# Attention over four images on one core: later column sums, a third forms buffer, one bias product, a new end, and matmul operands 320 bytes apart

## The chip, the core and the metric

The kernel runs on one core of a Trainium2 chip. A core has a matrix engine (PE, with its weight loads shown apart as PEld), a vector engine (DVE), an activation engine (ACT), a general engine (POOL) and a queue engine (SP). SP, ACT and POOL can also start DMA transfers. Each engine works through its own instructions in the order in which the program lists them, and semaphores make one engine wait for another. The metric is the time of one execution on the device, in microseconds (us).

## The reference

For each of B = 4 images with N = 64 * 64 = 4096 positions and C = 256 channels:

```python
q = x @ Wq + bq            # (N, 128)
k = x @ Wk + bk            # (N, 128)
v = x @ Wv + bv            # (N, 256)
pq, pk, pv = (t.reshape(B, -1, N) for t in (q, k, v))   # a reinterpretation of memory, no transpose
energy = einsum('bcn,bcm->bnm', pq, pk)                 # (N, N)
attention = softmax(energy, axis=-1)
out = einsum('bcm,bnm->bcn', pv, attention).reshape(x.shape)
result = gamma * out + x
```

All is float32. The kernel works without subtracting a maximum before the exponential. At its end it tests whether every column sum stayed within bounds, and a slower general path, behind a branch on that flag, would recompute everything. With these inputs the branch is not taken.

## The kernel before

**Forms.** A float32 operand of a matmul is split into three forms that the matrix engine reads in its rounded float32 type: h (the upper part, made by ACT), l (the rest) and d (a combination for the crossed terms), both made by DVE. A product of two numbers is then three matmuls, summed in PSUM: first the d forms, then, after the partial sum has been rescaled in place (`seed_qk`, `seed_v`, `cross`), the h and the l forms.

**Image 0** is projected first, in a loop over NI = 16 blocks `i` of 256 positions. The loop body is written out by hand, and this order holds on each engine:

- PE: `products(0, i, 0, (0, 1))` (8 matmuls for q and k), `products(0, i, 1, (0, 1))` (8 for v), then for block i + 1 the 4 d matmuls of q and k, the bias products `biased` (4 matmuls of a 128 x 128 tile of ones with the two forms of the bias), the 4 d matmuls of v, and 4 transposes of block i + 2.
- ACT: `qk_forms` (L268), `v_forms` (L152), `seed_qk` (L251), then `x_forms` of block i + 2 (L209) and, behind it, `seed_v` (L260, two instructions).
- DVE: two instructions each of `qk_forms` (L271) and `v_forms` (L155), then two of `x_forms` (L211, L213).
- POOL: four stores per block of the forms of q and k to DRAM (`store`, L290), and loads of q and k for the attention.

The forms of q and k of one block live in tile `f` of the ring `pf`, which has two buffers; L268 of block i overwrites the buffer of block i - 2, so it waits for that block's four stores.

**Attention** runs in B * 128 = 512 steps `n`; 16 steps (t = 0 to 15) make a group of 512 columns, and eight groups an image. On PE one step is `cross(n + 2)` (2 matmuls, L318), `attend(n, 0)` (6 matmuls, L378), `energy(n + 2)` (4 matmuls, L333) and `attend(n, 1)` (6 matmuls). ACT makes the rescaling (L319), the exponential (L336) and h (`upper`, L342); DVE the running column sum (L351), l (L356) and d (L358) in `halves(n + 1)`. Into the steps of images 0 to 2, `step` interleaves the projection of the next image: 24 product matmuls of 128 x 256 (L229) for each of its 16 blocks.

At the end of a group, ACT copies the accumulators out of PSUM (`emptied`, L392: half 0 in the last step, half 1 afterwards), PE adds the column sums over the partitions (`sums`, two matmuls, L416, into a bank that an accumulator of half 1 has held), and `finish` takes twelve pieces, one per step: the sums go through DRAM, are inverted, the output tile `o` is added up and multiplied, a POOL DMA adds x (L442) and an SP DMA stores the result (L446). In the last image `late` is 1: half 1 is emptied at t = 1 of the next group, and `sums` stands in the same step, right behind it.

`finish_last` is the end of the last group: column sums by four small float32 matmuls (`zp`, L459), reciprocal, a broadcast by a float32 matmul (`rp`, L478), the test of all sums (`np`, L481, and the flag `again`, L494), the scaling of the two halves and two stores (L488, L493). The branch on `again` (L675) follows.

Of the kernel before, what the change touches and what calls it, by code (L numbers as in the profile page):

```python
# [20 lines left out]
def kernel(  # L21
# [36 lines left out]
    nc = tc.nc  # L58
# [28 lines left out]
    LOOK = 2  # L87
    xg, og = columns(x, NB), columns(out, NB)
# [4 lines left out]
    again = const.tile([P, 1], I32, name="again")  # L93
    gam3 = const.tile([P, 3], F32, name="gam")
    gam, gam1, gam2 = (gam3[:, i : i + 1] for i in range(3))
    zs = const.tile([P, 1], F32, name="zs")
    rall = const.tile([P, B * NG, NJ], F32, name="rall")
    bias = const.tile([P, 2 * C2], F32, name="bias")
    bvs = const.tile([P, KC], F32, name="bvs")

    with ExitStack() as fast:
# [3 lines left out]
        )  # L105
        qkv = pool("qkv", 1)
# [10 lines left out]
        wf = qkv.tile([P, 2, 3, KC, C], F32R, tag="wf", name="wf")  # L117
# [32 lines left out]
        def split(h, l, d, y, scale=E):  # L150

            nc.scalar.activation(h, y, AF.Identity, scale=UPPER * scale)  # L152
            yield
            for t, f in ((d, 1.0 / scale + 1.0), (l, 1.0 / scale)):
                nc.vector.scalar_tensor_tensor(t, h.bitcast(F32), -f, y, ALU.mult, ALU.add)  # L155
                yield

        def weights(w):

            nc.scalar.mul(scaled[:, w], raw[:, w], E ** -(w + 1))  # L160
            yield from split(*(wf[:, w, f] for f in range(3)), scaled[:, w])
# [54 lines left out]
        def products(b, i, w, fs):  # L216
# [5 lines left out]
            for s in range(2):  # L222
                for f in fs:
                    for k in range(KC):
                        if w:
                            left, right = wf[:, 1, f, k, s * P : (s + 1) * P], xf[:, f, k]
                        else:
                            left, right = xf[:, f, k, s, :], wf[:, 0, f, k]
# [9 lines left out]
        def biased(i):  # L238

            to = units[0, 0, i]  # L240
            for f in range(2):
                for s in range(2):
                    nc.tensor.matmul(  # L243
                        to[:, s, :], ones_r, bf[:, f, :], start=False, stop=False,
                        skip_group_check=True,
                    )
# [17 lines left out]
        def qk_forms(b, i):  # L264
            y = units.pop((0, b, i))
            f = work.tile([P, 2, 3, C], F32R, tag="pf", name=f"f_{b}_{i}")
# [78 lines left out]
        def halves(n):  # L345
# [6 lines left out]
            else:  # L352
                now["s"] = x
            ld = ppool.tile([P, 2, 2, NB], F32R, tag="ld", name=f"ld_{n}")
# [6 lines left out]
            if n % NU == NU - 1:  # L361
                nc.vector.tensor_tensor(s[:, 0, :], s[:, 0, :], s[:, 1, :], ALU.add)
                now["sum"] = s
# [89 lines left out]
        def finish_last(n, xr):  # L453

            b, g = B - 1, NG - 1
            attend(n, 0)
# [21 lines left out]
            nc.tensor.matmul(rp, ones, work_[:, 0], start=True, stop=True)  # L478
# [408 lines left out]
```

## Time and profile before

| | us |
|---|---|
| median of 3 runs | 2398.16 (2396.82 to 2399.83) |
| the profiled execution | 2397.88 |
| its span, first to last instruction | 2396.1 |

Between the span and that execution's own time lie 1.8 us. A page of the profile gives the busy time of each engine, its share of the span, the costliest groups of instructions, and DMA. Other views answer questions about one stretch: a table of windows (busy time of each engine, the granted share of the PE clock, DMA), a timeline (start, duration, engine, line, output and inputs, how many instructions; in brackets the idle time before it and what ended it), and the chain of waits, followed back from the last instruction. A merged timeline row with xN spans from the start of the first of N instructions to the end of the last. PE matmuls are pipelined: one lasts longer than the distance to the next, so the spacing of N equal matmuls is (row's duration - one matmul's) / (N - 1).

### The profile page before, as it was taken

How to read it: one execution, taken by the hardware profiler on the slowest of the kernel's cores; microseconds unless marked ns; L12 is line 12 of the kernel's file. 1: busy time of each engine (PE TensorE's matmuls, PEld its weight loads, DVE VectorE, ACT ScalarE, POOL GpSimd, SP SyncE). 2: the span in 40 equal slices, each digit the busy share in tenths (PEclk: the TensorE clock that was granted, in tenths of full speed). 3: DMA queues.
4: the chain of work that ended last, by engine and by line, in shares of the span. 5: the costliest groups of instructions: out<-in, count | busy, mean ns of one | idle time of the engine just before them, and what ended most of it. 6: DMA issues, size and time to landing. Idle time of an engine off the chain costs nothing.

```text
span 2396.1 us, 31995 instructions
## 1 busy us (share of the span) xinstructions
PE 2355.5 (98%) x11158; PEld 1967.6 (82%) x11158; DVE 2135.3 (89%) x2111; ACT 1882.2 (79%) x3093; POOL 580.7 (24%) x943
## 2 busy tenths in 40 slices
PE   8999999999999999999999999999999999999998
PEld 7888888888888888888888888888888787777776
DVE  6889999999999999999999999999998888888887
ACT  6777788887888887888877888878887777777775
POOL 5422222222322222222232222222223111111110
PEclk9999999999999999999999999999999999999999
DMA  9857666567896576566697665676669545445443
GB/s 216 177 139 199 169 165 171 144 174 183 262 274 163 147 187 178 157 166 156 164 342 220 159 175 142 175 188 156 167 175 337 134 128 128 126 111 129 114 124 88
DMA packets 243991, 413.83 MB, mean 173 GB/s; under 512 B 26031, under 2 KB 141487, under 8 KB 243822
## 3 DMA queue, kind: packets, MB, share of 16 engines
q0 software_dynamic: 203152, 368.77, 59.2%
q1 hardware_dynamic: 40126, 42.67, 5.7%
q8 instruction: 91, 1.49, 0.3%
q14 instruction: 78, 0.64, 0.1%
q10 hardware_dynamic: 544, 0.26, 0.0%
HBM read 306.64 MB, written 104.98 MB: 172 GB/s over the span
## 4 chain that ended last, share of the span: by engine, by line
PE 96%; ACT 2%; DVE 1%; DMA 1%; issue 0%; POOL 0%; SPq 0%; ACTq 0%; DVEq 0%
PE a L378 39%; PE b L378 19%; PE e L333 19%; PE e L318 10%; PE qv L229 7%; PE xt L198 1%; PE z L416 1%; ACT x L336 0%; ACT o L392 0%; DMA qd<-f 0%; ACT qv L260 0%; DMA raw<-in_L_conv_Wv_dram 0%; PE qv L243 0%; ACT xf L209 0%; DVE ld L358 0%
## 5 line engine op out<-in xcount | busy, mean ns | idle before, releaser
L336 ACT ACTIVATE x<-e 128x512 f32<-128x512 f32 x960 | 522.0, 596 | 301.7 <-PE e L333 295.4
L305 POOL DMA_DIRECT2D k<-kf x512 | 275.5, 538 | 1738.3 <-PE e L333 1678.3
L356 DVE TENSOR_TENSOR ld<-x,h 128x1024 fp32r<-128x1024 f32 x480 | 586.0, 1221 | 100.5 <-ACT h L342 55.8
L351 DVE TENSOR_TENSOR s<-s,x 128x1024 f32<-128x1024 f32 x480 | 586.5, 1222 | 99.7 <-ACT x L336 97.5
L378 PE MATMUL a<-h,v 128*128 128x512 f32 x2048 | 642.9, 395 | 0.0
L319 ACT ACTIVATE e<-e 128x512 f32<-128x512 f32 x1024 | 546.4, 572 | 119.7 <-PE e L318 119.3
L378 PE MATMUL b<-ld,v 128*128 128x512 f32 x2048 | 632.7, 390 | 1.7 <-DVE f L271 1.5
L378 PE MATMUL a<-ld,v 128*128 128x512 f32 x2048 | 633.8, 391 | 0.0
L358 DVE SCALAR_TENSOR_TENSOR ld<-h,x 128x1024 fp32r<-128x1024 f32 x480 | 584.7, 1218 | 0.0
L333 PE MATMUL e<-q,k 128*128 128x512 f32 x2048 | 547.7, 389 | 0.0
L342 ACT ACTIVATE h<-x 128x1024 fp32r<-128x1024 f32 x480 | 510.5, 1064 | 13.2
L378 PEld LDWEIGHTS b<-ld,v 128*128 128x128 f32 x2048 | 384.8, 188 | 84.6 <-issue 1.9
L378 PEld LDWEIGHTS a<-ld,v 128*128 128x128 f32 x2048 | 385.4, 188 | 83.4
L333 PEld LDWEIGHTS e<-q,k 128*128 128x128 f32 x2048 | 384.2, 188 | 79.7
L378 PEld LDWEIGHTS a<-h,v 128*128 128x128 f32 x2048 | 369.5, 189 | 70.6 <-ACT o L392 7.3
L318 PE MATMUL e<-q,k 128*128 128x512 f32 x1024 | 316.2, 390 | 0.0
L318 PEld LDWEIGHTS e<-q,k 128*128 128x128 f32 x1024 | 192.2, 188 | 40.8
L229 PEld LDWEIGHTS qv<-xf,wf 128*128 128x128 f32 x768 | 107.5, 191 | 17.9 <-ACT qv L260 8.0
L229 PE MATMUL qv<-xf,wf 128*128 128x256 f32 x768 | 114.5, 285 | 7.2 <-ACT qv L260 5.4
L229 PE MATMUL qv<-wf,xf 128*128 128x256 f32 x768 | 114.9, 286 | 3.6 <-DVE xf L211 1.9
L229 PEld LDWEIGHTS qv<-wf,xf 128*128 128x128 f32 x768 | 108.1, 192 | 12.7 <-ACT qv L251 2.6
L290 POOL DMA_DIRECT2D kf<-f x128 | 98.3, 768 | 29.1 <-DVE f L271 6.9
(84 smaller groups left out, 1230.4 us busy)
## 6 DMA issues: line engine op xcount, KB each, us to landing
k<-kf POOLq DMA_DIRECT2D x512, 384.0 KB, 3.6
vf<-vf POOLq DMA_DIRECT2D x48, 768.0 KB, 5.3
v<-vf POOLq DMA_DIRECT2D x48, 768.0 KB, 8.3
kf<-f POOLq DMA_DIRECT2D x128, 192.0 KB, 4.4
qd<-f POOLq DMA_DIRECT2D x128, 192.0 KB, 4.4
q<-qd POOLq DMA_DIRECT2D x32, 768.0 KB, 5.2
o<-in_x_dram POOLq DMA_DIRECT2D x31, 512.0 KB, 7.4
out_dram<-o SPq DMA_DIRECT2D x31, 512.0 KB
```

Of the source, the lines that this page charges most:

```text
L229: nc.tensor.matmul(to[:, s, :], left, right.rearrange("p s a -> p (s a)") if w else right, start=(f == 2 and s == k == 0), stop=(f == 1 an ...
L290: nc.gpsimd.dma_start(to, f)
L305: nc.gpsimd.dma_start(t, kf[b, u % NU])
L318: nc.tensor.matmul(e, *forms(n, i, 2), start=True, stop=False, skip_group_check=True)
L319: nc.scalar.mul(e, e, -REST)
L333: nc.tensor.matmul(e, *forms(n, i, f), start=False, stop=(f == 1), skip_group_check=True)
L336: nc.scalar.activation(x[:, i, :], e, AF.Exp, scale=(1.0 + E) ** 3 / E)
L342: nc.scalar.activation(h, units[n], AF.Identity, scale=UPPER)
L351: nc.vector.tensor_tensor(s, s, x, ALU.add)
L356: nc.vector.tensor_tensor(l, x, h.bitcast(F32), ALU.subtract)
L358: nc.vector.scalar_tensor_tensor(d, h.bitcast(F32), 1.0 + E, x, ALU.mult, ALU.subtract)
L378: nc.tensor.matmul(to, vall[:, t, f, i, j * P : (j + 1) * P], units[n][f][:, i, :], start=(t == 0 and i == 0 and f != 1), stop=(t == NU - ...
```

## The change

- `sums` and the start of `finish` move in the last image from t = 1 to t = 2 of the next group (`t == 2 * late`).
- In image 0 the forms of every third block go into a third tile, `f3`, which is the not yet used first buffer of the ring `q`.
- `biased` issues 2 matmuls rather than 4: the bias's upper part stands in partition 0 and its rest in partition 32 of one 64-row operand that is zero elsewhere.
- In the loop of image 0, `seed_v(0, i + 1)` stands right behind its products, ahead of the transposes and of `x_forms(0, i + 2)` on ACT.
- At the start, the scaling of the raw weights moves from ACT to DVE, and ACT makes h from the raw weights.
- The matmuls of `products` run over forms, then contraction halves, then output halves `s` (before: `s` outermost).
- Tiles move: the weights' forms become two tiles, small tiles stand between them, and x's forms get their own pool behind 192 bytes of padding (in image 0 they start 192 bytes into the buffer `ld`). By the addresses of the built programs, stationary minus moving operand of `products` was a multiple of 512 bytes and is 320 bytes modulo 512 afterwards. All other matmuls of the attention keep a multiple of 512; the tile of ones stood and stands 384 (modulo 512) from the bias's form and from the forms of the column sums.
- The end: the last column sum is added up ahead of the last l and d; the small matmuls, the broadcast and the test stand ahead of both last `attend` halves or between them; the flag `again` is computed before the last multiplications, and each engine reads it at the end of its own work; the last half takes one DVE instruction less.

```diff
+    PAD = 48
...
+        wf = [pool("wqk", 1).tile([P, 3, KC, C], F32R, name="wqkf")]
+        small = pool("small", 1)
...
+        wf.append(pool("wv", 1).tile([P, 3, KC, C], F32R, name="wvf"))
...
+        pool("pad", 1).tile([P, PAD], F32, name="pad")
+        xpool = pool("xf", 1)
...
         def weights(w):
-            nc.scalar.mul(scaled[:, w], raw[:, w], E ** -(w + 1))
-            yield from split(*(wf[:, w, f] for f in range(3)), scaled[:, w])
+            y, c = scaled[:, w], E ** -(w + 1)
+            nc.vector.tensor_scalar(y, raw[:, w], c, None, ALU.mult)
+            h, l, d = (wf[w][:, f] for f in range(3))
+            nc.scalar.activation(h, raw[:, w], AF.Identity, scale=UPPER * E * c)
...
             if b == 0:
-                f = ppool.tile([P, 3, KC, 2, P], F32R, tag="ld", name=f"xf_{b}_{i}")
+                f = ppool.tile([P, PAD + 6 * C], F32R, tag="ld", name=f"xf_{b}_{i}")
+                f = f[:, PAD:].rearrange("p (f k s a) -> p f k s a", f=3, k=KC, s=2)
             else:
-                f = work.tile([P, 3, KC, 2, P], F32R, tag="xf", name=f"xf_{b}_{i}", bufs=1)
+                f = xpool.tile([P, 3, KC, 2, P], F32R, tag="xf", name=f"xf_{b}_{i}")
...
-            for s in range(2):
-                for f in fs:
-                    for k in range(KC):
+            for f in fs:
+                for k in range(KC):
+                    for s in range(2):
...
         def biased(i):
-            for f in range(2):
-                for s in range(2):
-                    nc.tensor.matmul(
-                        to[:, s, :], ones_r, bf[:, f, :], start=False, stop=False,
-                        skip_group_check=True,
-                    )
+            for s in range(2):
+                nc.tensor.matmul(
+                    to[:, s, :], ones_r[:64], bf[:64], start=False, stop=False,
+                    skip_group_check=True,
+                )
...
+            if b == 0 and i % 3 == 2:
+                f = f3
+            else:
+                f = work.tile([P, 2, 3, C], F32R, tag="pf", name=f"f_{b}_{i}")
...
+            if n == B * STEPS - 1:
+                whole()
             ld = ppool.tile([P, 2, 2, NB], F32R, tag="ld", name=f"ld_{n}")
...
         def finish_last(n, xr):
-            attend(n, 0)
             zp = ps_e.tile([P, NJ], F32, tag="e", name="zp")
...
+            attend(n, 0)
             emptied(n, 0)
             o = now["o"]
-            attend(n, 1, (2,))
             rp = ps_e.tile([P, NB], F32, tag="e", name="rp")
             nc.tensor.matmul(rp, ones, work_[:, 0], start=True, stop=True)
-            attend(n, 1, (0, 1))
             np_ = ps_p.tile([P, 1], F32, tag="p0", name="np")
             nc.tensor.matmul(np_, ones, zs, start=True, stop=True)
-            nc.scalar.activation(o[:, 1, 1, :], now["b", 1], AF.Identity, scale=gam1)
+            attend(n, 1, (2, 0, 1))
             r = work.tile([P, NB], F32, tag="r", name="r_last", bufs=1)
             nc.scalar.copy(r, rp)
+            nc.scalar.activation(o[:, 1, 1, :], now["b", 1], AF.Identity, scale=gam1)
             nc.vector.tensor_tensor(o[:, 0, 0, :], o[:, 0, 0, :], o[:, 1, 0, :], ALU.add)
+            nc.vector.tensor_scalar(again, np_, P - 0.5, None, ALU.is_lt)
...
-            nc.vector.tensor_tensor(o[:, 1, 1, :], o[:, 1, 1, :], r, ALU.mult)
-            nc.vector.tensor_tensor(xr[:, 1, :], xr[:, 1, :], o[:, 1, 1, :], ALU.add)
-            nc.vector.scalar_tensor_tensor(o[:, 0, 1, :], now["a", 1], gam2, r, ALU.mult, ALU.mult)
-            nc.vector.tensor_tensor(xr[:, 1, :], xr[:, 1, :], o[:, 0, 1, :], ALU.add)
+            y = o[:, 1, 1, :]
+            nc.vector.scalar_tensor_tensor(y, now["a", 1], gam2, y, ALU.mult, ALU.add)
+            nc.vector.tensor_tensor(y, y, r, ALU.mult)
+            nc.vector.tensor_tensor(xr[:, 1, :], xr[:, 1, :], y, ALU.add)
             nc.sync.dma_start(og[b, g][:, 1], xr[:, 1, :])
-            nc.vector.tensor_scalar(again, np_, P - 0.5, None, ALU.is_lt)
...
+        f3 = work.tile([P, 2, 3, C], F32R, tag="q", name="f3")
...
                 products(0, i + 1, 1, (2,))
+                seed_v(0, i + 1)
             if i + 2 < NI:
                 transposed(0, i + 2)
                 xs = x_forms(0, i + 2)
                 next(xs)
-            if i + 1 < NI:
-                seed_v(0, i + 1)
...
-            if t == late and n > 1:
-                sums(n - 1 - late)
+            if t == 2 * late and n > 2:
+                sums(n - 1 - 2 * late)
                 active.append(finish(n // NU - 1, now["o"], now["total"]))
...
+        unsafe = nc.values_load(again[0:1, 0:1])
...
-    with tc.If(nc.values_load(again[0:1, 0:1]) > 0), ExitStack() as general:
+    with tc.If(unsafe > 0), ExitStack() as general:
```

More of the change, by code (lines that the diff above doesn't have):

```diff
@@ L105 @@
         )
+        wf = [pool("wqk", 1).tile([P, 3, KC, C], F32R, name="wqkf")]
+        small = pool("small", 1)
+        bvs = small.tile([P, KC], F32, name="bvs")
+        zs = small.tile([P, 1], F32, name="zs")
+        gams = small.tile([P, 2], F32, name="gams")
+        gam1, gam2 = gams[:, :1], gams[:, 1:]
+        both = small.tile([P, 2], F32, name="both")
+        gam, again = both[:, :1], both[:, 1:].bitcast(I32)
+        wf.append(pool("wv", 1).tile([P, 3, KC, C], F32R, name="wvf"))
         qkv = pool("qkv", 1)
@@ L353, in halves, with whole @@
                 now["s"] = x
+            def whole():
+                nc.vector.tensor_tensor(s[:, 0, :], s[:, 0, :], s[:, 1, :], ALU.add)
+                now["sum"] = s
+            if n == B * STEPS - 1:
+                whole()
             ld = ppool.tile([P, 2, 2, NB], F32R, tag="ld", name=f"ld_{n}")
@@ L360, in halves @@
             )
-            if n % NU == NU - 1:
-                nc.vector.tensor_tensor(s[:, 0, :], s[:, 0, :], s[:, 1, :], ALU.add)
-                now["sum"] = s
+            if n % NU == NU - 1 and n < B * STEPS - 1:
+                whole()
             units[n] = h, l, d
@@ L551 @@
         image(0)
+        f3 = work.tile([P, 2, 3, C], F32R, tag="q", name="f3")
         for i in range(4):
             load_x(0, i)
[L554 to L555 removed]
+        bf = xpool.tile([P, 3, KC, 2, P], F32R, tag="xf", name="bf")
+        bf, bh = (bf[:, 0, k].rearrange("p s a -> p (s a)") for k in range(KC))
+        nc.vector.tensor_scalar(bf[:64], zs[:64].to_broadcast([64, C]), 0.0, None, ALU.mult)
         transposed(0, 0)
```

32 lines of the change are left out of this document (14 added, 18 removed).

## The prediction

> **What bounds the kernel now.** I read the table of windows first (columns: stretch, its length, busy us of PE, PEld, DVE, ACT and POOL, granted PE clock, DMA share, GB/s).
>
> ```profile
> span 2396.1 us, 31995 instructions
> ...
> 17.08:83.59 66.51, 59.39 (x463) 55.93 (x461) 51.57 (x83) 47.76 (x94) 46.54 (x62) 1.00 1.17 246
> ...
> 40.00:60.00 20.00, 17.27 (x134) 16.05 (x133) 13.99 (x23) 13.62 (x28) 13.20 (x19) 1.00 1.34 302
> ...
> 600.00:1200.00 600.00, 600.00 (x2855) 501.58 (x2855) 549.25 (x542) 484.00 (x793) 150.01 (x243) 1.00 0.69 185
> ...
> 1800.00:2300.00 500.00, 486.86 (x2136) 400.93 (x2135) 427.65 (x385) 387.90 (x630) 84.77 (x149) 0.99 0.55 150
> ...
> 1842.00:1850.00 8.00, 6.12 (x20) 4.58 (x19) 4.98 (x5) 4.59 (x9) 1.06 (x2) 0.79 0.87 292
> ...
> 2117.00:2125.00 8.00, 6.46 (x21) 5.18 (x22) 4.57 (x4) 4.51 (x8) 0.50 (x1) 0.79 0.18 50
> ...
> 2390.00:2396.10 6.10, 0.00 (x0) 0.00 (x0) 0.00 (x0) 0.00 (x0) 0.00 (x0) 0.50 0.06 14
> ```
>
> Four stretches with four limits. While attention and projection run together (600 to 1200) PE never rests: there only a shorter matmul spacing saves time. In image 0 (17 to 84) no engine is full, so a chain through several of them is the limit. In the last image (from 1800) PE loses 13 of 500 us. At the end nothing shown as busy runs for the last 6.1 us.
>
> **Image 0.** The timeline of one block:
>
> ```profile
> 20.14 1.22 PE L229 MATMUL qv<-xf,wf 128*128 128x256 f32 x8 [0.54 <-ACT qv L260]
> ...
> 21.68 0.63 PE L243 MATMUL qv<-bf,ones 128*128 128x256 f32 x4
> 22.15 0.64 PE L229 MATMUL qv<-xf,wf 128*128 128x256 f32 x4
> 22.63 0.60 PE L198 MATMUL xt<-ident,xs 128*128 128x128 f32 x4
> ...
> 23.27 0.60 ACT L209 ACTIVATE xf<-xt 128x512 fp32r<-128x512 f32 x1 [0.33 <-PE xt L198]
> 23.76 0.93 ACT L260 ACTIVATE qv<-qv,bvs 128x256 f32<-128x256 f32 x2
> ...
> 24.74 1.01 PEld L229 LDWEIGHTS qv<-xf,wf 128*128 128x128 f32 x8 [0.74 <-ACT qv L260]
> ...
> 49.20 0.63 PE L243 MATMUL qv<-bf,ones 128*128 128x256 f32 x4
> ...
> 51.14 0.60 ACT L268 ACTIVATE f<-qv 128x512 fp32r<-128x512 f32 x1 [3.52 <-DMA qd<-f]
> ...
> 55.62 0.63 PE L243 MATMUL qv<-bf,ones 128*128 128x256 f32 x4
> ```
>
> From 20.14 to 24.74 one block takes 4.60 us, along one chain: v's products, next d products, bias, transposes, L209, L260, v's products again. L260 needs only v's d products (done near 22.8) but queues behind L209, which waits for the transposes. With `seed_v` ahead, L209 and L260 (1.4 us) no longer stand between transposes and products; PE's q and k products run beside L260. What is late next is DVE: 51.57 us of work in the 14 blocks from 17.08 to 83.59, 3.7 per block; PE needs 24 products and 2 bias matmuls at 0.12 and 4 transposes at 0.11, 3.55. So 66.5 us become at best 51.6 plus what DVE waits at the `cross` and `energy` blocks; I take 55.5, **a gain of 11**. The two bias matmuls saved (0.24 per block) are worth nothing here, since DVE's 3.7 hides them; without that cover they would give 15 x 0.24 = 3.6 more.
>
> The third buffer: one block (49.20 to 55.62) takes 6.42 because L268 waits 3.52 for the stores of two blocks before. Three buffers add a block of slack, so this 1.8 goes (it is in the 11), and without them the shorter block could not be had: stores would be late in every block. `f3` is the buffer that the second load of q takes, in step 6 of the attention, long after block 14's stores. The limit of all this is DMA: 66.51 us at 246 GB/s are 16.4 MB, at the 302 GB/s of 40 to 60 that is 54.2 us. This is the upper end of the gain, 12.3; if only 270 GB/s come, 60.6 us, a gain of 6.
>
> **The start.**
>
> ```profile
> 7.76 0.63 ACT L160 ACTIVATE scaled<-raw 128x512 f32<-128x512 f32 x1 [1.36 <-DMA raw<-in_L_conv_Wv_dram]
> ...
> 9.09 1.29 DVE L155 SCALAR_TENSOR_TENSOR wf<-wf,scaled 128x512 fp32r<-128x512 f32 x2 [1.85 <-ACT wf L152]
> ...
> 11.50 0.42 DVE L563 SCALAR_TENSOR_TENSOR bf<-bias,bf 128x256 fp32r<-128x256 f32 x1
> ```
>
> Moving the scaling to DVE puts the second scaling, which waits for Wv at 7.76, ahead of all forms on DVE's queue. Before, DVE did four instructions of 0.6 from 9.09 and the bias form from 11.50 to 11.92. Afterwards the scaling ends at 7.76 + 0.63 = 8.4 if DVE takes as long for it as ACT, and then six of 0.61 follow, to 12.1 (the two that ran at 6 us before now stand behind it), and two on one partition each, for which I allow 0.2: the bias form is ready at 12.5. Two bias matmuls fewer on the path give 0.24 back: **+0.4** (0 to 1).
>
> **Products in images 1 to 3.** Timeline rows for the spacing, and from the groups by line (busy us, mean ns) how long one matmul lasts:
>
> ```profile
> 602.54 1.12 PE L229 MATMUL qv<-wf,xf 128*128 128x256 f32 x8
> 603.50 0.63 PE L416 MATMUL z<-zf,ones 128*128 128x512 f32 x2
> 608.22 0.64 PE L229 MATMUL qv<-xf,wf 128*128 128x256 f32 x4
> ...
> L229 PE MATMUL qv<-xf,wf 128*128 128x256 f32 x204 | 29.8, 282 | 0.0
> ...
> L333 PE MATMUL e<-q,k 128*128 128x512 f32 x2048 | 547.7, 389 | 0.0
> ...
> 2356.13 1.07 PE L333 MATMUL e<-q,k 128*128 128x512 f32 x4
> ```
>
> Spacing now: (1.12 - 0.28) / 7 = 0.120 and (0.64 - 0.28) / 3 = 0.120. The trace has no operands 320 bytes apart. The same shape with 384 is the bias product (21.68, and 0.28 for one): (0.63 - 0.28) / 3 = 0.117. The lower bound is the transposes (22.63, likewise), (0.60 - 0.28) / 3 = 0.11, where the weight load alone sets the pace. On the other side, 128x512 matmuls keep (1.07 - 0.39) / 3 = 0.227 with a multiple of 512, and the pair of column sums, 384 apart, 0.63 - 0.39 = 0.24 or less: up to 0.01 worse. 3 x 16 x 24 = 1152 products times 0.003, the nearest row, are **3.3 saved**; bounds 11.5 saved and 6 lost (half of 0.01, those being twice as long). The order by alternating halves alone I cost at nothing: PE is full with either order, and the rows of L333, which change tile after every second matmul, keep the same 0.227. If each change of half cost 0.005, it would be 5.8.
>
> The Trainium skill ("SBUF — State Buffer", section "SBUF: two separate sides") says that PE has ports of its own and waits on no one, with separate ones for the stationary and the moving operand; by it, the distance of the operands is worth 0 and the total 3.3 higher, and 0.117 beside 0.120 does not refute it.
>
> **The last image.** Around t = 1 of its last group, and the view of waits by tile:
>
> ```profile
> 2320.88 1.07 PE L333 MATMUL e<-q,k 128*128 128x512 f32 x4
> 2321.53 1.08 ACT L336 ACTIVATE x<-e 128x512 f32<-128x512 f32 x2 [0.93 <-PE e L333]
> ...
> 2322.50 0.69 ACT L392 ACTIVATE o<-a,gam 128x512 f32<-128x512 f32 x1
> 2323.07 0.70 ACT L392 ACTIVATE o<-b,gam 128x512 f32<-128x512 f32 x1
> 2323.64 1.08 ACT L342 ACTIVATE h<-x 128x1024 fp32r<-128x1024 f32 x1
> 2323.83 0.73 PE L416 MATMUL z<-zf,ones 128*128 128x512 f32 x2 [1.88 <-ACT o L392]
> ...
> L416 PE MATMUL z<-zf,ones x16: 389/497/690, 1845.4 to 2324.2; 128*128 128x512 f32 x16
> ```
>
> 16 matmuls, so eight such waits. The four of L333 are issued by 2321.79, z at 2323.83: 2.04 us lost, 8 x 2.04 = 16.3. One step later L392 is long done. The pair itself, 0.73 after the pause against 0.63 at 603.50, gives 0.8 more. And the clock: in two of the windows above it is 0.79 over 8 us around such a wait, 8 x 0.21 = 1.7 us of pace each, part of it inside the wait; I take 1.5 each, 3.0. Together 20.1.
>
> The Trainium skill ("TensorE: Matmul & The Clock Gate", "What's actually happening") lets the clock fall only after an idle window of about 3.4 us; here 2.0 us were enough in two of eight cases, so the measurement decides. By the page the 3.0 would not come back, total 3.0 higher.
>
> What is late next: behind L392 on ACT stand L342 and the next rescalings L319. Without PE's pause, L319 would start at 2324.6 (L342 begins 2323.64), end its first half at 2325.2, while PE, back from two `attend` halves of 1.36 from 2321.79 and two `cross` of 0.45, wants it at 2324.96. So a wait of 0.3 takes the place: 8 x 0.3 = 2.6, **net 17.5**. From below it is 0; from above the whole 1.27 of L392, 10.
>
> The copy of the sums on ACT, the pieces of `finish`, its SP transfers and POOL's L442 all come 4.1 us later. L442 also moves behind the group's last load of k, which by then waits for nothing new.
>
> ```profile
> 2365.59 0.54 SPq L446 DMA_DIRECT2D out_dram<-o  x1
> ...
> 2377.64 0.69 DVE L362 TENSOR_TENSOR s<-s 128x512 f32<-128x512 f32 x1
> ...
> 2378.55 0.69 ACT L392 ACTIVATE o<-a,gam 128x512 f32<-128x512 f32 x1 [3.26 <-PE a L378]
> ...
> 2381.61 2.07 PE L478 MATMUL rp<-last,ones 128*128 128x512 f32 x2 [0.43 <-DVE last L466]
> ...
> 2388.39 0.15 DVE L494 TENSOR_SCALAR again<-np 128x1 int32<-128x1 f32 x1
> 2388.50 0.34 SPq L493 DMA_DIRECT2D out_dram<-xr  x1
> ```
>
> The store of `o` (2365.59) would go out at 2369.7, 9 us before L392 overwrites `o` at 2378.55: covered.
>
> **The end.** Before, the last column sum (2377.64) is added after l and d, and PE, out of `attend`, waits for the reciprocal chain; `rp`, run after a pause, takes 2.07. Afterwards the sum is added 2.3 earlier. My estimate: PE does the small matmuls from 2377.2 (1.8), `attend` half 0 until 2380.4 (six at 0.227), `rp` and `np` (1.4), then half 1 until 2383.2. DVE's last five instructions of 0.7, the first beside the end of half 1, end at 2385.8, the second store goes at 2385.9, not 2388.50: 2.6. The flag, 2388.39 before, falls at 2382.7; the branch of most engines then runs beside the last multiplications. If the 7.6 us of tail hang on the store alone, the gain is 2.6; if on the flag alone, 5.7. I take **4.0**.
>
> **Sum.** 11 - 0.4 + 3.3 + 17.5 + 4.0 = 35.4 off the profiled execution's 2397.88 (span plus 1.8), which is 0.3 under the median: 2362.5.
>
> **Rivals.**
> 1. The distance clears the whole overhead: products at 0.11, 8.2 more: 2354. For it: every product shows the same 0.120, as if by rule. Against: 0.117 at 384.
> 2. It does nothing, as the page has it: 2366.
> 3. Another resource takes image 0 or the last image: DMA at 270 GB/s (5 less), or L319 waiting for all of L392 (8 less): 2368 to 2375. For it: a DMA share over 1.
> 4. Slower: at 320 the two reads of PE collide more. It would decide from 32 / 1152 = 0.028 on, products at 0.148; at 0.16, 2397.9 - 32.1 + 46 = 2412. Nothing over 0.01 is in the rows.
>
> **Chances.** Forecast 0.50, rival 1 0.18, rival 2 0.15, rival 3 0.13, rival 4 0.04. The range, 2350 to 2375, leaves out rival 4 and the far end of rivals 1 and 3. A measurement here tells 0.2% (4.8 us) from nothing: faster 0.94, same 0.02, slower 0.04.
>
> **What the next profile would show.** No wait of z for L392, L319 0.3 late instead, clock 1.00 until the last group; block spacing in image 0 of 3.8 to 4.0 with DVE nearly full; bias form near 12.5; products near 0.117; at the end the flag ahead of the first store, and `rp` in about 1 us, not 2. Products outside 0.11 to 0.125, or block spacing over 4.3, would make the number wrong.

## The result, and the profile after

The changed kernel takes 2371.64 us (median of 4 runs, 2370.47 to 2372.89). The kernel before, with one run more than above, has a median of 2398.95. The ratio is 0.9888, with a 95% interval from 0.987 to 0.9905: 1.1% faster, some 27 us. The forecast was 2362.5 us, within 2350 to 2375. So the sign and the range held, and the gain was 27 us where 35 were forecast. The profiled execution took 2371.13 us with a span of 2369.3, which is 26.8 less than the span before.

To see where the 26.8 us come from, I mark three points in both traces: the energy matmuls (four to a row) of the 17th step, of the first step of the last image and of the last step. From the timeline of the kernel before, with two bias rows of image 0:

```profile
17.08 0.63 PE L243 MATMUL qv<-bf,ones 128*128 128x256 f32 x4
83.59 0.63 PE L243 MATMUL qv<-bf,ones 128*128 128x256 f32 x4
152.12 1.07 PE L333 MATMUL e<-q,k 128*128 128x512 f32 x4
1830.17 1.07 PE L333 MATMUL e<-q,k 128*128 128x512 f32 x4
2372.45 1.07 PE L333 MATMUL e<-q,k 128*128 128x512 f32 x4
```

The same five places in the changed kernel:

```profile
18.15 0.59 PE L255 MATMUL qv<-bf,ones 64*128 64x256 f32 x2
77.61 0.50 PE L255 MATMUL qv<-bf,ones 64*128 64x256 f32 x2
145.59 1.07 PE L348 MATMUL e<-q,k 128*128 128x512 f32 x4
1824.29 1.07 PE L348 MATMUL e<-q,k 128*128 128x512 f32 x4
2349.97 1.07 PE L348 MATMUL e<-q,k 128*128 128x512 f32 x4
```

| stretch | before | after | change | forecast |
|---|---|---|---|---|
| start and image 0, to the first mark | 152.12 | 145.59 | -6.5 | -10.6 |
| images 1 to 3 projected, first to second mark | 1678.05 | 1678.70 | +0.65 | -3.3 |
| last image, second to third mark | 542.28 | 525.68 | -16.6 | -17.5 |
| end, third mark to the end of the span | 23.65 | 19.33 | -4.3 | -4.0 |

So 4.1 of the 8.6 us that are missing lie in image 0, and 4.0 in the products. The last image and the end came within 1 us.

In image 0, the 66.51 us between the two bias rows have become 59.46, 7.0 less. The table of windows of the changed kernel (columns as before: length, busy us of PE, PEld, DVE, ACT, POOL, granted PE clock, DMA share, GB/s):

```profile
20.00:40.00 20.00, 20.00 (x148) 17.91 (x147) 17.38 (x29) 15.16 (x30) 14.41 (x20) 1.00 1.19 233
...
1800.00:2300.00 500.00, 499.01 (x2198) 410.27 (x2197) 439.00 (x394) 399.92 (x652) 85.03 (x150) 1.00 0.55 149
```

In the last image PE's loss has gone from 13 us in 500 to 1, and its clock is 1.00. In image 0 PE is now shown as busy all the time, and DVE for 17.4 of 20 us: it isn't DVE that sets the pace. (One of these matmuls lasts 0.28 us and the next can start 0.12 after it, so short waits of PE don't show as idle time.) The timeline of one block:

```profile
28.49 0.59 ACT L222 ACTIVATE xf<-xt 128x512 fp32r<-128x512 f32 x1
...
29.11 0.69 DVE L224 SCALAR_TENSOR_TENSOR xf<-xf,xt 128x512 fp32r<-128x512 f32 x1 [0.42 <-ACT xf L222]
...
29.86 0.74 PE L242 MATMUL qv<-wqkf,xf 128*128 128x256 f32 x4
...
30.53 0.50 PE L255 MATMUL qv<-bf,ones 64*128 64x256 f32 x2
...
30.96 0.74 PE L242 MATMUL qv<-xf,wvf 128*128 128x256 f32 x4
31.07 0.58 ACT L263 ACTIVATE qv<-qv 128x512 f32<-128x512 f32 x1 [0.53 <-PE qv L255]
...
31.74 0.93 ACT L272 ACTIVATE qv<-qv,bvs 128x256 f32<-128x256 f32 x2
...
32.59 0.59 ACT L222 ACTIVATE xf<-xt 128x512 fp32r<-128x512 f32 x1
```

From 28.49 to 32.59 one block takes 4.10 us, and a new chain has taken the place of the old one: h of x (L222), d of x (L224), d products of q and k, bias, d products of v, `seed_v` (L272), and h of x for the next block behind it on ACT. The rescaling (L263) runs beside the d products of v; L272 starts when these end, at 30.96 + 0.74 = 31.70. The chain runs through the bias matmuls, and these have become slower, not faster: the two of 64 rows start 0.67 us after the d products of q and k, and v's start 0.43 us after them, although only half as many are issued. They lengthen PE's own queue by as much as the chain, and PE is nearly full, so the trace alone doesn't tell which of the two sets the 4.10.

### The profile page after: what moved, and what is told of

Same layout as the page of the kernel before. It is cut to its first block, busy times and chain, and to the rows that moved or that the text cites. A ratio compares the mean times of both kernels' runs of the same rounds, so it can differ in the third digit from the quotient of the medians.

```text
span 2369.3 us, 31941 instructions
## 1 busy us (share of the span) xinstructions
PE 2351.7 (99%) x11126; PEld 1960.3 (83%) x11126; DVE 2136.3 (90%) x2114; ACT 1881.0 (79%) x3091; POOL 580.6 (25%) x943
## 4 chain that ended last, share of the span: by engine, by line
PE 97%; ACT 1%; DVE 1%; issue 0%; DMA 0%; SPq 0%; DVEq 0%; ACTq 0%
PE a L398 39%; PE e L348 20%; PE b L398 19%; PE e L333 10%; PE qv L242 8%; PE xt L210 1%; PE z L436 1%; ACT o L412 0%; ACT x L351 0%; PE qv L255 0%; ACT e L334 0%; DMA raw<-in_L_conv_Wv_dram 0%; ACT h L357 0%; DVE ld L379 0%; DVE f L286 0%
## 5 line engine op out<-in xcount | busy, mean ns | idle before, releaser
L334 ACT ACTIVATE e<-e 128x512 f32<-128x512 f32 x1024 | 546.7, 573 | 109.1 <-PE e L333 108.4
L348 PE MATMUL e<-q,k 128*128 128x512 f32 x2048 | 548.7, 390 | 1.1
L348 PEld LDWEIGHTS e<-q,k 128*128 128x128 f32 x2048 | 383.0, 188 | 84.4 <-ACT e L334 6.0
L333 PE MATMUL e<-q,k 128*128 128x512 f32 x1024 | 316.6, 390 | 0.0
L333 PEld LDWEIGHTS e<-q,k 128*128 128x128 f32 x1024 | 191.7, 188 | 41.0
L242 PE MATMUL qv<-wqkf,xf 128*128 128x256 f32 x768 | 115.4, 287 | 4.0 <-DVE xf L224 4.0
L242 PEld LDWEIGHTS qv<-wqkf,xf 128*128 128x128 f32 x768 | 107.8, 192 | 13.7 <-DVE xf L224 4.9
L242 PEld LDWEIGHTS qv<-xf,wvf 128*128 128x128 f32 x768 | 107.2, 191 | 10.2 <-ACT s L437 0.7
L242 PE MATMUL qv<-xf,wvf 128*128 128x256 f32 x768 | 114.3, 285 | 0.3 <-ACT s L437 0.3
```

The source lines that it names most:

```text
L242: nc.tensor.matmul(to[:, s, :], left, right.rearrange("p s a -> p (s a)") if w else right, start=(f == 2 and s == k == 0), stop=(f == 1 an ...
L333: nc.tensor.matmul(e, *forms(n, i, 2), start=True, stop=False, skip_group_check=True)
L334: nc.scalar.mul(e, e, -REST)
L348: nc.tensor.matmul(e, *forms(n, i, f), start=False, stop=(f == 1), skip_group_check=True)
```

## The experiments

All times are medians of 4 or 5 runs. Differences of a microsecond between kernels that ran at different times are not resolved by them; there the marks in the traces decide.

**The bias over 128 rows.**

```diff
-                    to[:, s, :], ones_r[:64], bf[:64], start=False, stop=False,
+                    to[:, s, :], ones_r, bf, start=False, stop=False,
...
-        nc.vector.tensor_scalar(bf[:64], zs[:64].to_broadcast([64, C]), 0.0, None, ALU.mult)
+        nc.vector.tensor_scalar(bf, zs.to_broadcast([P, C]), 0.0, None, ALU.mult)
```

> The changed kernel, with the two bias matmuls over all 128 rows (the 62 rows that carry nothing hold zeros) instead of over 64. Theory A (the trace of the changed kernel): the blocks of image 0 follow one chain, x_forms L222, L224, d products of q and k, bias, L263, L272, x_forms again, 4.10 us; and the 64-row matmuls start 0.207, 0.222 and 0.205 us apart from their neighbours, where full ones take 0.12. Then the three distances fall to about 0.12 each, the block to 3.8 to 3.9 us, and the time by 3 to 5 us. Theory B (the forecast): DVE or DMA sets the block and hides the bias; then the time stays within 1 us. Theory C: a pair of matmuls into two halves of one bank is slow whatever its rows; then the distances stay at 0.2 us and so does the time.

2367.26 us, 4.4 less than the changed kernel. The timeline of a block of this kernel:

```profile
28.50 0.74 PE L242 MATMUL qv<-wqkf,xf 128*128 128x256 f32 x4
...
29.08 0.40 PE L255 MATMUL qv<-bf,ones 128*128 128x256 f32 x2
...
29.31 0.64 PE L242 MATMUL qv<-xf,wvf 128*128 128x256 f32 x4
...
32.22 0.74 PE L242 MATMUL qv<-wqkf,xf 128*128 128x256 f32 x4
```

Bias follows 0.58 after the d products, v's d products 0.23 after the bias, and these take 0.64 and not 0.74: together 0.39 us less than with 64 rows, for the same number of matmuls. The block falls from 4.10 to 3.72 us, by the same 0.38. That is theory A, with the block a little under its 3.8 to 3.9, and B and C are out. Now DVE is nearly full:

```profile
20.00:40.00 20.00, 20.00 (x162) 19.14 (x161) 19.47 (x32) 16.28 (x33) 16.48 (x23) 1.00 1.35 269
```

Not every block gains. By the marks image 0 ends 3.7 us earlier (141.87 for 145.59), not 15 x 0.38 = 5.7: five later blocks take 22.3 us together (44.0 to 66.2), where the changed kernel's take 22.5 (46.9 to 69.4), and in the first of them L283 waits 1.54 us (until 49.40) for stores of q again.

Against the four full matmuls of before (21.68 to 22.15 in the prediction's rows, 0.47 for the group) the two 64-row ones saved 0.04 and lost 0.09 ahead of them and 0.10 behind them.

The Trainium skill ("TensorEngine Tiling (Array Packing)", section "Key Properties") states that a change of the tiling mode, not only of the tile, drains the TensorE. The traces are in line with it: four distances, into, within and behind the 64-row pair, are about 0.1 us longer each, 0.39 together, and they shrink to 0.11 to 0.12 when all rows are used. That a drain is what takes the time no run here shows. The prediction overlooked this rule.

**`seed_v` back in its place.**

```diff
                 products(0, i + 1, 1, (2,))
-                seed_v(0, i + 1)
             if i + 2 < NI:
                 transposed(0, i + 2)
                 xs = x_forms(0, i + 2)
                 next(xs)
+            if i + 1 < NI:
+                seed_v(0, i + 1)
```

> The changed kernel, with seed_v back behind the transposes and x_forms. Theory A (a chain sets the block): L272 again waits behind L222 and v's products behind both; block 4.5 to 4.7 us as before the change, time +6 to +8 us. Theory B (the forecast: DVE sets the block, and moving seed_v was worth the whole of the 11 us but the 1.8 of the third buffer): +9 us. Theory C (the third buffer and DMA set the block): within 2 us of the changed kernel.

2377.01 us: 5.4 more, a little under theory A's 6 to 8. The chain of before is there again, with v's products waiting for L272 and blocks of 4.72 us (28.43 to 33.15):

```profile
28.43 0.60 ACT L222 ACTIVATE xf<-xt 128x512 fp32r<-128x512 f32 x1 [0.53 <-PE xt L210]
...
29.90 1.20 PE L242 MATMUL qv<-xf,wvf 128*128 128x256 f32 x8 [0.57 <-ACT qv L272]
...
33.15 0.60 ACT L222 ACTIVATE xf<-xt 128x512 fp32r<-128x512 f32 x1 [0.53 <-PE xt L210]
```

So the move is worth 5.4 us with the slow bias (5.2 by the marks: image 0 ends at 150.80). That the old order is at 4.72 here and was at 4.60 before the change is again the bias, 0.12 to 0.15 us in either chain.

**Without the third buffer.**

```diff
-            if b == 0 and i % 3 == 2:
-                f = f3
-            else:
-                f = work.tile([P, 2, 3, C], F32R, tag="pf", name=f"f_{b}_{i}")
+            f = work.tile([P, 2, 3, C], F32R, tag="pf", name=f"f_{b}_{i}")
```

> The changed kernel, without the third forms buffer (ring of two in image 0). Theory A (the stores of two blocks before come in time as long as DMA keeps up, and are late at one or two blocks only): L283 waits 1 to 4 us in one or two blocks of image 0 and the time rises by 1 to 4 us. Theory B (the forecast: without it the stores would be late in every block): block period back above 4.4 us and +5 us or more. Theory C (the buffer is worth nothing at a block of 4.1 us): within 1 us.

2378.49 us: 6.9 more, above A's range, though not in every block as B has it. The groups by line from 18 to 95 us of this kernel, where the h of q and k is L280 (last columns: busy us, mean ns, idle time before it and what ended it), from its timeline the longest of these waits, and from its table of windows image 0:

```profile
L280 ACT ACTIVATE f<-qv 128x512 fp32r<-128x512 f32 x16 | 9.6, 598 | 12.7 <-DMA qd<-f 8.4 <-PE qv L242 4.2
```

```profile
53.17 0.60 ACT L280 ACTIVATE f<-qv 128x512 fp32r<-128x512 f32 x1 [5.69 <-DMA qd<-f]
```

```profile
18.00:78.00 60.00, 56.07 (x385) 50.10 (x383) 45.80 (x75) 41.91 (x83) 39.87 (x53) 0.93 1.12 241
```

The same group of the changed kernel:

```profile
L283 ACT ACTIVATE f<-qv 128x512 fp32r<-128x512 f32 x15 | 9.0, 599 | 1.3 <-PE qv L242 1.2
```

The 8.4 us of waiting for stores are gone with the third buffer. One wait of 5.69 us makes up most of it, behind the first load of q on the same queue (issued at 41.22); before the change the same wait was 3.52 us. Part of the price is the clock: the granted share of 0.93 is a stretch at 0.50 from 53.1 to 59.9 us, right behind the long wait. The third buffer doesn't end the waits for good: in six of the other runs that have it, L283 still waits 1.3 to 1.9 us in all for stores of q, nearly all of it in the ninth or tenth block.

**The distance of 320 bytes.** The small tiles stand ahead of the weights' forms, and the padding goes; stationary minus moving operand is then a multiple of 512 again.

```diff
-    PAD = 48
+    PAD = 0
...
-        wf = [pool("wqk", 1).tile([P, 3, KC, C], F32R, name="wqkf")]
         small = pool("small", 1)
...
+        wf = [pool("wqk", 1).tile([P, 3, KC, C], F32R, name="wqkf")]
         wf.append(pool("wv", 1).tile([P, 3, KC, C], F32R, name="wvf"))
...
-        pool("pad", 1).tile([P, PAD], F32, name="pad")
```

> The changed kernel, with the operands of the products again a multiple of 512 bytes apart (the small tiles stand ahead of the weights' forms, no padding); loop order by alternating halves kept. Theory A (the distance is worth nothing): spacing of the products in images 1 to 3 stays at 0.1175, time within 1 us. Theory B (the distance is what brought the steady spacing from 0.120 to 0.1175): spacing back to 0.120, 1152 x 0.0025 = +2.9 us. Theory C (alternating halves need the distance): more than 0.120 and +3 to +10 us.

2371.03 us. **The order of the loops** alone:

```diff
-            for f in fs:
-                for k in range(KC):
-                    for s in range(2):
+            for s in range(2):
+                for f in fs:
+                    for k in range(KC):
```

> The changed kernel, with the output halves s outermost in the products again; distance 320 kept. Theory A (the order is worth nothing): spacing stays 0.1175 and the time within 1 us. Theory B (alternating halves brought 0.120 to 0.1175): +2.9 us. Theory C (the distance alone is worth more, and alternating the halves costs some of it back): spacing 0.110 to 0.115 and the time 3 to 8 us lower.

2371.96 us. Neither median stands apart from the changed kernel's 2371.64. The traces tell more. Rows of eight products, and the two marks, of the kernel with distance 0:

```profile
145.44 1.07 PE L347 MATMUL e<-q,k 128*128 128x512 f32 x4
...
606.11 1.12 PE L241 MATMUL qv<-xf,wvf 128*128 128x256 f32 x8
...
1823.58 1.07 PE L347 MATMUL e<-q,k 128*128 128x512 f32 x4
```

and of the kernel with the old order:

```profile
146.70 1.07 PE L348 MATMUL e<-q,k 128*128 128x512 f32 x4
...
607.54 1.10 PE L242 MATMUL qv<-xf,wvf 128*128 128x256 f32 x8
...
1825.41 1.07 PE L348 MATMUL e<-q,k 128*128 128x512 f32 x4
```

At 320 bytes the row takes 1.10 (in the changed kernel too, at 606.41), at 0 it takes 1.12, in either order. Over all products between 200 and 1800 us the mean distance from one start to the next is 0.1185 at 0 and 0.1177 at 320. So theory B is right about which part moves the spacing, the distance and not the order, but the size is 0.9 ns and not 2.5: some rows of products begin with a spacing of 0.113 at distance 0, so that its mean is well below the steady 0.120. And the gain is given back: from mark to mark the kernel with distance 0 takes 1678.14 us, with the old order 1678.71, and the changed kernel 1678.70 (1678.43 to 1678.74 in the eight other runs at 320 bytes). With 320 bytes the rest of PE's work is 1.6 us slower, that is 0.56 and the 1152 x 0.0009 that the products save; the single records put it on some starts beside the products' steps (from `attend` to `cross` 2 ns more on the mean, from the column sums to `attend` 12). Why these suffer from tiles that they don't read stays open.

**The later sums alone**, in the kernel before:

```diff
-            if t == late and n > 1:
-                sums(n - 1 - late)
+            if t == 2 * late and n > 2:
+                sums(n - 1 - 2 * late)
```

> The kernel before, with only the later column sums of the last image (t == 2 * late). Theory A (the trace of the changed kernel: 2.04 us of waiting and the two half-clock stretches go, a wait of 0.41 us for the rescaling comes in each of eight groups): 16 to 17 us less than before, 2381.5 to 2383. Theory B (the gain depends on other parts of the change, such as the moved tiles or the end): less than 13 us. Theory C (the forecast, 17.5): 2381.

2381.34 us, 16.6 less than the 2397.89 of the kernel before in the same comparison (ratio 0.9931, 0.9918 to 0.9945): theory A. The marks of the last image are 525.52 us apart, 525.68 in the changed kernel:

```profile
1830.97 1.07 PE L333 MATMUL e<-q,k 128*128 128x512 f32 x4
...
2356.49 1.07 PE L333 MATMUL e<-q,k 128*128 128x512 f32 x4
```

The part works by itself and needs nothing of the rest.

**The copy split.** In the changed kernel the wait that was forecast for L319 (now L334) is there, around t = 1 of each group:

```profile
1838.15 0.69 ACT L412 ACTIVATE o<-a,gams 128x512 f32<-128x512 f32 x1
...
1839.29 1.08 ACT L357 ACTIVATE h<-x 128x1024 fp32r<-128x1024 f32 x1
...
1840.24 1.10 ACT L334 ACTIVATE e<-e 128x512 f32<-128x512 f32 x2
...
1840.91 0.30 PEld L348 LDWEIGHTS e<-q,k 128*128 128x128 f32 x2 [0.56 <-ACT e L334]
...
1841.95 0.63 PE L436 MATMUL z<-zf,ones 128*128 128x512 f32 x2
```

PE loses 0.30 us ahead of L348 and 0.11 within it (single records 0.529 and 0.337 us apart where 0.227 is usual). The column sums behind it wait for nothing.

```diff
             if t == late and n > 1:
-                emptied(n - 1 - late, 1, done)
+                emptied(n - 1 - late, 1, done, (1,) if late else (0, 1))
+            if late and t == 3 and n > 3:
+                emptied(n - 4, 1, done, (0,))
```

> The changed kernel; in the last image the copy of the two accumulators of half 1 (L412) is split, the one whose bank the column sums need at t = 1, the other at t = 3, instead of both at t = 1. Theory A (the waits of 0.41 us of L348 for the rescaling L334 in each of its groups come from the 1.2 us that L412 takes ahead of it on ACT): half of it fits beside PE, the waits go, and the time falls by 7 or 8 x 0.41 = 2.9 to 3.3 us. Theory B (another wait takes their place, on the copy of the sums L437 or on L351): less than 1 us.

2369.82 us. In its trace the waits are gone: PE is busy for all of the 500 us (table of windows), and the last image takes 522.43 us from mark to mark (timeline), 3.25 less than in the changed kernel, some 8 x 0.41. By the marks that is theory A.

```profile
1800.00:2300.00 500.00, 500.00 (x2213) 413.86 (x2213) 441.62 (x397) 401.32 (x655) 86.41 (x153) 1.00 0.56 151
```

```profile
1825.61 1.07 PE L348 MATMUL e<-q,k 128*128 128x512 f32 x4
...
2348.04 1.07 PE L348 MATMUL e<-q,k 128*128 128x512 f32 x4
```

The median shows 1.8 of it; the profiled run reached the last image 1.3 us later than the changed kernel's did. Nothing in this edit touches image 0, so that is how much image 0 differs between executions of the same code: the second pair of bias matmuls starts 0.66 us later, and in the ninth block, 0.77 us longer, L283 waits 1.63 us for stores, where the changed kernel's profile has no such wait.

**The start.**

```diff
         transposed(0, 0)
+        for _ in range(9):
+            nc.tensor.matmul(wp, ones, ones, start=True, stop=True)
```

> The changed kernel, with nine more matmuls of no use (the tile of ones with itself) behind the first transposes, which fill PE's pause of 4.0 us at 5 to 9 us. Theory A (the pause is why the granted clock of the profiled run is 0.50 until 18 us, and the start loses 1.1 us by it): granted clock 1.00 from about 9 us on, first blocks 1 to 2 us earlier and the time 1 to 2 us lower. Theory B (the loss at the start is DVE's longer queue ahead of the bias form): within 0.5 us, whatever the clock.

2371.48 us, no difference, as theory B has it. The granted clock (the third number from the end) stayed at 1.00 until 10.9 us, not 8.1 as in the changed kernel (0.53 from 8 to 10), and was then 0.50 until 17.7, not 18.4. From 10.8 to 12.5 us PE stands still again, waiting for the bias form:

```profile
8.00:10.00 2.00, 0.53 (x4) 0.53 (x4) 2.00 (x5) 0.78 (x2) 0.00 (x0) 1.00 0.88 292
...
12.00:14.00 2.00, 1.49 (x7) 1.24 (x7) 0.42 (x2) 0.66 (x2) 1.55 (x4) 0.50 0.00 0
```

So a clock of 1.00 from 9 us on, theory A's condition, did not come about, and what it would be worth stays untested.

**The end of before** in the changed kernel (`finish_last`, the place of the last sum and of the flag):

```diff
+            attend(n, 0)
             zp = ps_e.tile([P, NJ], F32, tag="e", name="zp")
...
-            attend(n, 0)
             emptied(n, 0)
...
+            attend(n, 1, (2,))
             rp = ps_e.tile([P, NB], F32, tag="e", name="rp")
             nc.tensor.matmul(rp, ones, work_[:, 0], start=True, stop=True)
+            attend(n, 1, (0, 1))
             np_ = ps_p.tile([P, 1], F32, tag="p0", name="np")
             nc.tensor.matmul(np_, ones, zs, start=True, stop=True)
-            attend(n, 1, (2, 0, 1))
...
             nc.sync.dma_start(og[b, g][:, 1], xr[:, 1, :])
+            nc.vector.tensor_scalar(again, np_, P - 0.5, None, ALU.is_lt)
```

> The changed kernel with the end of the kernel before (the last column sum behind l and d, attend half 0 ahead of the small matmuls, the flag behind the second store, four instructions of DVE for the last half, the flag read in front of the branch). Theory A (the forecast and the trace of the changed kernel: from the last step's energy matmuls to the end of the span 4.3 us less): 4.0 to 4.5 us slower than the changed kernel. Theory B (the tail hangs on the second store alone): 2.6 us slower. Theory C (it hangs on the flag alone): 5.7 us slower.

2374.44 us: 2.8 more by the medians, 3.4 by the traces (2372.8 of span against 2369.3, with the last step 0.12 later), under theory A's 4.0 to 4.5. The end of the old order:

```profile
2359.24 1.13 PE L497 MATMUL rp<-last,ones 128*128 128x512 f32 x2 [0.43 <-DVE last L485]
...
2365.19 0.34 SPq L512 DMA_DIRECT2D out_dram<-xr  x1
```

and of the changed kernel:

```profile
2358.09 1.02 PE L497 MATMUL rp<-last,ones 128*128 128x512 f32 x2
...
2359.73 0.15 DVE L505 TENSOR_SCALAR both<-np 128x1 int32<-128x1 f32 x1
...
2363.48 0.34 SPq L513 DMA_DIRECT2D out_dram<-xr  x1
```

Part of the gain is the second store, 1.6 us earlier; from it to the end of the span are 5.8 us instead of 7.6, which is the other 1.8. It goes with the earlier flag and the place where it is read; this edit moves the two together. Neither B nor C is right alone. The 0.9 that are missing to the 4.3 between the two kernels are the half clock of before: without the waits for the column sums, `rp` takes 1.13 us in the old order too, not 2.07.

**Two versions put together.** The first has the bias over 128 rows, the split copy, and at the start

```diff
-        for pieces in first:
-            next(pieces)
         nc.vector.tensor_copy(bf[:1], bh[:1].bitcast(F32))
         nc.vector.tensor_tensor(bf[32:33], bias[32:33], bh[32:33].bitcast(F32), ALU.subtract)
+        for pieces in first:
+            next(pieces)
```

> The changed kernel with bias matmuls over 128 rows, the split copy of half 1 in the last image, and DVE's two bias instructions at the start ahead of the three l forms. Theory A (the parts add up: bias 4.4, split 1.8 to 3.3, and 0.5 to 1.2 for the earlier bias form at the start): 2363 to 2365 us. Theory B (the l forms, now 0.7 us later, hold up the first products as much as the bias form did): 2365 to 2366 us.

2362.49 us, ratio to the kernel before 0.985 (0.9834 to 0.9867): faster than both kernels, 9 us under the changed one and a little under theory A's 2363 to 2365. The second pair of bias matmuls starts at 16.14 us, at 18.15 in the changed kernel:

```profile
16.14 0.40 PE L255 MATMUL qv<-bf,ones 128*128 128x256 f32 x2
```

Of these 2.0 us, 0.8 are the bias form's place on DVE, for the first pair starts at 11.35 instead of 12.12. The other 1.2 go with the clock, which reaches 1.00 at 15.0 us here and at 18.4 in the changed kernel; whether the earlier bias form brings that about is not shown. The second version also takes `seed_v` out of image 0's new chain:

```diff
                 seed_qk(0, i + 1)
+                if i + 2 < NI:
+                    transposed(0, i + 2)
+                    xs = x_forms(0, i + 2)
+                    next(xs)
                 products(0, i + 1, 1, (2,))
                 seed_v(0, i + 1)
```

> As best1, and in image 0 the transposes and x_forms stand ahead of v's d products and seed_v, which takes L272 (0.85 us) out of the chain L222, L224, d products, bias, L263. Theory A (the chain still sets the block of 3.7 us that the 128-row bias left): block 3.5 to 3.6 us, and 1.5 to 3 us less than best1. Theory B (DVE's 3.6 us, or the DMA's stores, set the block by now): within 1 us of best1. Theory C (v's products now wait for L272): blocks longer, +1 us or more.

2362.62 us, the same as the first (theory B as to the time). The blocks are not the same: most take 3.72 us in the first version and 3.89 in this one, for v's products now wait for L272, as theory C has it. One of these weight loads, with the next such wait at 25.43:

```profile
21.54 0.98 PEld L242 LDWEIGHTS qv<-xf,wvf 128*128 128x128 f32 x8 [0.34 <-ACT qv L272]
```

What the blocks lose, the start gives back: the second pair of bias matmuls comes at 15.24 instead of 16.14. At 3.72 us a block DVE is busy for 19.8 of the 20 us from 20 to 40 in the first version, and the chain and PE lie so near to it that this order gains nothing.

## Why the prediction was right or wrong

**Image 0: the direction right, 4.1 us too much.** The step that failed is "What is late next is DVE", and within it the term "2 bias matmuls at 0.12": with 64 rows they lengthen PE's block by 0.39 us more than that, as the run with 128 rows shows. PE then needs not 3.55 us a block but, by these distances, 3.94, more than DVE's 3.7, and DVE is busy for 17.4 of 20 us only. Moving `seed_v` ahead took L209 and L260 out of the way of v's products, as said, but it also put L260 ahead of L209 on ACT, so that the x forms of the next block wait for it, and this chain runs through the same bias matmuls. The sentence that asked what is late next looked only at how busy the engines are, and not at what the moved instruction now stands in front of. The block took 4.10 us; 3.8 to 4.0 had been named, and 4.3 as the point where the number is wrong. Whether the chain or PE's queue holds it at 4.10 stays open, since the bias lies on both.

So two bias matmuls fewer were not worth nothing, hidden by DVE: with 64 rows they cost 0.15 us a block more than the four before. Over all 128 rows they bring 4.4 us (3.7 by the marks). Then DVE is busy for 19.5 of 20 us, the stretch from the second to the last bias pair takes 55.9 us (17.92 to 73.78) where 55.5 had been forecast, and the limit named is the right one. The third buffer was worth 6.9 us and not a side condition; that without it there is no shorter block was right in the sum, though a few long waits and a stretch at half the clock, and not every block, showed it.

**The start: the queue right, the rest not the change's.** +0.4 (0 to 1) was forecast. The first pair of bias matmuls started at 12.12 us, 0.15 later than before (11.97),

```profile
12.12 0.79 PE L255 MATMUL qv<-bf,ones 64*128 64x256 f32 x2 [1.00 <-DVE bf L585]
```

right behind the form, which was ready at 12.06 and not at the 12.5 of the forecast. The next pair came 1.07 us later than before, and the other 0.9 are the clock. The d products of q and k just ahead of that pair, before and after:

```profile
16.61 0.64 PE L229 MATMUL qv<-wf,xf 128*128 128x256 f32 x4
...
17.17 1.05 PE L242 MATMUL qv<-wqkf,xf 128*128 128x256 f32 x4
```

At the start, products stand 0.213 us apart, and 0.118 later; the step lies at 16.1 us before and at 18.4 in the changed kernel, whose granted clock goes from 0.50 to 1.00 there (the profile of before has no clock on record ahead of 16.1). This moment differs between executions: it is 16.1 and 17.9 us in the two profiles with the old start, and 15.7 to 19.0 in the eight with the new one. So the 0.9 can't be put down to the change.

**Products: wrong.** The step is "1152 products times 0.003, the nearest row". The spacing came out as forecast, 0.117, but the 0.120 it was to be compared with is that of one row; the mean of all before was 0.1185. The true term is 1152 x 0.0009 = 1.0. And "PE is full with either order" was taken to mean that nothing else moves: 1.6 us came back elsewhere. Rival 2, that the distance does nothing, is right as to this term. The Trainium skill's rule of separate ports ("SBUF — State Buffer", "SBUF: two separate sides") gave the better number for the total; the distance does shift the spacing by 0.9 ns, in a way that the rule has no word for. The order by alternating halves is worth nothing, as costed.

**The last image: right.** 16.6 of 17.5. The eight waits of 2.04 (16.3) and the two half-clock stretches are gone: by the starts of the same matmuls in each group, 1.66 us are saved in most groups, and 3.3 in the two that held a stretch, so 1.6 for each where 1.5 was taken. The wait that takes their place is at the place named, L319 behind L392 and L342, and is 0.41 (3.3 for eight), because the second pair of L333 waits as well. The prediction took 2.6 for eight, though its own figures, 2325.2 and 2324.96, give 0.24 each, or 1.9. Of the 0.8 for the pair of column sums some 0.3 showed: the step with the sums took 6.69 us before and takes 4.61 where nothing waits (the split copy), 2.08 less, so 16.6 for eight and not 16.3 + 0.8. The Trainium skill's idle window of about 3.4 us ("TensorE: Matmul & The Clock Gate", "What's actually happening") would have left the 3.0 unsaved; the measurement disagrees, with 3.3 saved.

**The end: right.** 4.3 for 4.0, between the bounds of 2.6 and 5.7. The second store goes 2.5 us earlier after the last step's mark, as forecast (2.6), but 0.9 of that is `rp` at the full clock and 1.6 the new order; the other 1.8 is the shorter way from the store to the end.

The forecast lay 9 us under the measured time, and the range held it because rival 3's and rival 2's ends were in it; as to image 0 that is luck, since neither rival names the bias. Rival 3's causes were not the main cause: in the changed kernel's profile no wait of L283 for a store is left in image 0 (six other runs have 1.3 to 1.9 us of it), and L319 waits for a third of L392 and not for all of it.

## What to carry to other kernels

When an instruction is moved forward on an engine's queue, follow what it now stands in front of around the whole loop, and not only how full the engines are: the new chain is found by walking once round it with the durations in hand. Count a matmul by the distance from its neighbours and not by its rows; one that uses fewer rows than those around it can cost more than two full ones. And compare a spacing with the mean over all such instructions, for a single row of eight can be 1% off, which is all that is at stake here. The start of a kernel is a poor place to compare two profiles by a microsecond: here the clock alone moved it by more, between kernels whose start is the same or nearly so.

## What the runs showed of the hardware

- Two matmuls of 64 rows among matmuls of 128 start 0.207, 0.222 and 0.205 us apart from their neighbours, and the second one after them 0.227; with 128 rows all these distances are 0.11 to 0.12.
- The same products in another place of the memory, 320 instead of 0 bytes modulo 512 between the operands, are 0.9 ns closer, and other matmuls, which don't read these tiles, get slower by 1.6 us in total, where the products save 1.0.
- Nine matmuls in a pause kept the granted clock at 1.00 until 10.9 us instead of 8.1, and it was 0.50 at 12 to 14 in either kernel.
- At the start the granted clock reached 1.00 at 15.7 to 19.0 us in eight profiles whose start is the same or nearly so. In image 0, a wait of 5.69 us for stores was followed by a stretch at 0.50 from 53.1 to 59.9 us.
